# A planner that counts VectorE's pauses one behind the other, and inverse roots of eleven instructions

## The chip, the cores and the metric

The program runs on one core of one Trainium2 chip. The metric is the time of one execution on the device in microseconds (us). Five engines work side by side, each through its own list of instructions in the order in which the program emitted them: TensorE (PE, with PEld for the loading of weights), VectorE (DVE), ScalarE (ACT), GpSimd (POOL) and SyncE (SP), which starts most transfers.

## The reference

Two transformer blocks run one after the other over x, which is 2 x 1024 rows of 256, with 16 heads of 16.

- Block 1: norm, self-attention, residual; norm, cross-attention to 64 rows of context, residual; then a mixture of 8 experts. A router takes the two best experts of each row, each expert is a layer of 1024 with gelu, and the two answers are added with their gates.
- Block 2: norm, self-attention, residual; norm, cross-attention with a mask, residual; norm, a dense layer of 1024 with gelu, residual.

A norm in both blocks is (x - mean) / sqrt(var + 1e-5), then scale and shift:

```python
def _ln(x, g, b):
    m = x.mean(-1, keepdims=True)
    v = ((x - m) ** 2).mean(-1, keepdims=True)
    return (x - m) / jnp.sqrt(v + EPS) * g + b
```

## The kernel before

**Tiles and stages.** x lies in on-chip memory as 16 tiles of 128 rows. Four tiles are a unit, numbered 0 to 3, so that units 2 and 3 are the second batch. Self-attention runs in 128 cells a block (head by head, 128 keys to a cell), in which TensorE, VectorE (maxima of the scores) and ScalarE (exp) work in step. Everything else of the block is cut into steps which are put between the cells, and the steps that are left after the last cell run in a drain.

**What sets the order.** Four of the engines run in the order of emission, and the emission is planned in Python by `Stream`. A job is a generator (`Task`) which emits a few instructions and yields. A positive number is TensorE time that these take, a negative number a pause in which the job is not to be asked for its next step. `step` chooses between the cells, where a pause is rounded up to whole cells of 3.3 us. `rest` chooses in the drain: it keeps a clock `now` that only the positive numbers move, and takes of the jobs whose pause is over the one with the highest rank. A pause there begins at `now`, whatever else VectorE was given. None of these numbers reaches the chip. They set the order, and the chip's semaphores then hold each instruction until its data are there.

`rest` serves three stretches: the drain behind block 1's cells, the stretch in which block 2 begins while the last expert jobs run, and the drain behind block 2's cells.

**The jobs of block 1's drain**, with the lines by which the profile knows them:

- *Cross norm of unit 3* (`norm_task`, rank 67): `statistics` of four tiles on VectorE (L402, L403, tiles `st_c`, `mv_c`), `inverse_roots` (L385 to L393, `root_c`, `rs_c`), `center`, which makes the normed rows (L416, `xn_c`), and their turning on TensorE (L428) and ScalarE (L435). A pause of 3.4 stands behind the roots and one of 1.8 behind the first two tiles of `center`. At the end POOL adds a bias to x (L488).
- *Ask, weigh and share of unit 3* (ranks 30, 30, 50): queries (L1303), four groups of scores with their maxima (L1345 on TensorE, L1353, L1366 and L1367 on VectorE), `largest` (L1372), `weights` (L1382 and L1388, exp on ScalarE at L1393), `undivided` (L1442, L1452), `division` (L1467), and the output (L496, added to x at L504).
- *Dispatch of units 2 and 3* (`dispatch_task`, rank 70, tiles named `_m`): the same statistics and roots, the rows `xd_m` (L1576), their turning (L428), the router (L1589, L1599), the best two experts (L1602 to L1621, in two steps), the counts (L1629 to L1650), the gates (from L1655, with an exp at L1656), the places (L1675, L1676, two steps), and eight scattering transfers by POOL (L1684).
- *Find* (`find` with `Places.make`, rank 65): six small VectorE steps (L1697 to L1812) that say which expert each slot of 256 rows serves. SP then reads the numbers and fetches weights (L1872) and rows (L1864).
- *Slots 0 to 4* (ranks 10 to 6): turning of the fetched rows (L1934) with seven small VectorE instructions (L1940 to L1957), `first0` to `first3` (L1969, gelu on ScalarE at L1975), and four halves of `second` (L2000). Slot 0 may begin when units 0 and 1 are counted, the others when unit 2 is.
- *Context of block 2* (rank -20), which fills gaps (L1223, L1245).
- The last heads of self-attention (L888 to L914) and their projection (L496), on which the cross norm of unit 3 waits.

Fourteen instructions make the roots: two for a first guess, then three rounds of four. `helper()` gives POOL while `maxima[0]` is true, which is as long as VectorE has maxima to take, and VectorE after that.

Of the kernel before, what the change touches and what calls it, by code (L numbers as in the profile page):

```python
# [43 lines left out]
I32 = mybir.dt.int32  # L44
U32 = mybir.dt.uint32
AF = mybir.ActivationFunctionType
ALU = mybir.AluOpType
# [5 lines left out]
B, S, D, H, DH = 2, 1024, 256, 16, 16  # L53
# [5 lines left out]
EPS = 1e-5  # L59

GUESS = 0x5F3759DF
# [3 lines left out]
CELL = 3.3  # L65
# [66 lines left out]
W_B1, W_1, W_2, W_B2 = 0, 8, 2056, 4104  # L132
NFF = 4360

class Task:


# [7 lines left out]
class Stream:  # L145
# [63 lines left out]
                self.advance(t)  # L209
        assert mark in self.made, mark  # L210

    def rest(self, later, cell, mark=None):

        now, ready = 0.0, {t: (t.first - cell) * CELL for t in self.tasks}
        while (self.tasks or later) and (mark is None or mark not in self.made):
            for c in sorted(later):
                if (c - cell) * CELL <= now:
                    for go in later.pop(c):  # L220
                        go()
            tasks = [t for t in self.tasks if self.made.issuperset(t.after)]
            able = [t for t in tasks if ready.get(t, 0.0) <= now]
            if able:
                t = max(able, key=lambda t: (t.rank, -ready.get(t, 0.0)))
                cost = self.advance(t)
                if cost is not None:
                    now += max(0.0, cost)
                    ready[t] = now - min(0.0, cost) + (t.pause or 0.0)
            else:  # L230
                now = min([ready[t] for t in tasks] + [(c - cell) * CELL for c in later])
        return now
# [3 lines left out]
def two_blocks(  # L236
# [16 lines left out]
    nc = tc.nc  # L253
    const = ctx.enter_context(tc.tile_pool(name="const", bufs=1))
# [87 lines left out]
    def choice(layer, pool):  # L342
        for b in range(1 + layer):
            chosen[layer].append(pool.tile([P, 2, P], F32R, name=f"chosen{layer}{b}"))
# [26 lines left out]
    maxima = [True]  # L371
# [6 lines left out]
    def inverse_roots(rs, var, tag, pool, engine):  # L378


        n = rs.shape[1]
        v, r = [
            pool.tile([P, 8], F32, tag="root", name=f"root{i}_{tag}", bufs=4)[:, :n] for i in range(2)
        ]
        engine.tensor_scalar(v, var, EPS, None, ALU.add)  # L385
        engine.tensor_scalar(
            rs.bitcast(I32), v.bitcast(I32), -0.5, float(GUESS), ALU.mult, ALU.add
        )
        for _ in range(3):
            engine.tensor_tensor(r, rs, rs, ALU.mult)  # L390
            engine.tensor_tensor(r, r, v, ALU.mult)
            engine.tensor_scalar(r, r, -0.5, 1.5, ALU.mult, ALU.add)
            engine.tensor_tensor(rs, rs, r, ALU.mult)  # L393

    def statistics(src, nt, tag, pool=small, each=False, engine=None):


        st = pool.tile([P, 8, 6], F32, tag="st", name=f"st_{tag}", bufs=4)
        mv = pool.tile([P, 8, 2], F32, tag="mv", name=f"mv_{tag}", bufs=6)
        rs = pool.tile([P, 8], F32, tag="rs", name=f"rs_{tag}", bufs=6)  # L400
        for t in range(nt):
            nc.vector.bn_stats(st[:, t, :], src(t))  # L402
            nc.vector.bn_aggr(mv[:, t, :], st[:, t, :])  # L403
            if each or t % 2 == 1:
                yield -1.2
        inverse_roots(rs[:, :nt], mv[:, :nt, 1], tag, pool, engine or helper())
        yield -3.4 if engine is None else -4.4
        return mv, rs

    def center(src, pair, held, tag, pool=small):  # L410
# [30 lines left out]
    def norm_task(first, nt, ln, dst, tag, pool=small, held=None, engine=None):  # L441


        def src(t):
            return x_sb[:, first + t, :]

        if held is None:
            held = yield from statistics(src, nt, tag, pool, engine=engine)
        nxt = center(src, (0, 1), held, tag, pool)
        yield -1.8  # L450
        for t0 in range(0, nt, 2):
            xns, nxt = nxt, None
            if t0 + 2 < nt:
                nxt = center(src, (t0 + 2, t0 + 3), held, tag, pool)
            i, tp = turned(xns)
            affine(dst[:, :, t0 * P : (t0 + 2) * P], i, tp, ln)
            yield 1.0, 1.8
# [1105 lines left out]
    def dispatch_task(unit, pool, counted):  # L1563
# [7 lines left out]
        mv, rs = yield from statistics(src, 4, name)  # L1571
# [5 lines left out]
                xd[:, t, :D], src(t), mv[:, t, 0:1], rs[:, t : t + 1], ALU.subtract, ALU.mult  # L1577
            )
        lg = small.tile([P, 4, E], F32, tag="lg", name=f"lg_{name}")
        yield -5.0 if maxima[0] else -1.8  # L1580
        hT = pool.tile([P, 2, 512], F32, tag="dh", name=f"hT_{name}")
        for t0 in range(0, 4, 2):
            i, tp = turned([xd[:, t0 + n, :D] for n in range(2)])
# [26 lines left out]
        for k in range(2):  # L1610
            hot = hots[k]
            nc.vector.tensor_reduce(mx[:, k, :], lg, AX.X, ALU.max)
            nc.vector.tensor_tensor(hot, lg, mx[:, k, :].unsqueeze(2).to_broadcast(shape), ALU.is_equal)
            nc.vector.tensor_tensor(hot, hot, desc_b, ALU.mult)
            first = small.tile([P, 4], F32, tag="first", name=f"first_{name}{k}")
            nc.vector.tensor_reduce(first, hot, AX.X, ALU.max)
            nc.vector.tensor_tensor(hot, desc_b, first.unsqueeze(2).to_broadcast(shape), ALU.is_equal)
            yield -1.0
            if k == 0:
                nc.vector.scalar_tensor_tensor(lg, hot, -3.0e38, lg, ALU.mult, ALU.add)  # L1620
                nc.vector.tensor_scalar(  # L1621
                    xd[:, :, D + M_E0], first, -1.0, float(E), ALU.mult, ALU.add
                )
# [17 lines left out]
        else:  # L1641
# [1 line left out]
                before, before, inside.unsqueeze(2).to_broadcast([P, E, 4]), ALU.add  # L1643
            )
            nc.vector.tensor_tensor(inside, inside, upto[:, :, 3], ALU.add)
        yield -1.2
        i, pk = bank()
        pk = pk[:, : E * 4]
        nc.tensor.matmul(pk, lhsT=tri, rhs=chosen.rearrange("p e t -> p (e t)"), start=True, stop=False)
# [23 lines left out]
        for k in range(2):  # L1673
            mine = small.tile([P, 4, E], F32, tag="mine", name=f"mine_{name}{k}")
            nc.vector.tensor_tensor(mine, hots[k], place.rearrange("p e t -> p t e"), ALU.mult)  # L1675
            nc.vector.tensor_reduce(at[:, k, :], mine, AX.X, ALU.max)  # L1676
            yield -0.5
        counted()

        for t in range(4):  # L1680
# [36 lines left out]
    class Places:  # L1717
# [3 lines left out]
        def make(self, pool, name, n, had, caps, last):  # L1721
# [18 lines left out]
            nc.vector.memset(begin[:, m:], 0.0)  # L1740
            nc.vector.tensor_copy(end[:, : m - E], begin[:, E:m])
            nc.vector.tensor_copy(end[:, m - E :], caps[-1])
            yield -0.9
            upto = pool.tile([P, m], F32, tag="ntu", name=f"ntu_{name}", bufs=1)
            nc.vector.tensor_tensor(upto, end, begin[:, :m], ALU.subtract)
            nc.vector.tensor_tensor_scan(upto, ones[:, :m], upto, 0.0, ALU.mult, ALU.add)
# [17 lines left out]
                ALU.is_ge,  # L1764
            )
            self.who = const.tile([P, n], F32, name=f"who_{name}")
            yield -0.9
            row = pool.tile([P, n], F32, tag="row", name=f"row_{name}", bufs=1)
            past = pool.tile([P, n], F32, tag="past", name=f"past_{name}", bufs=1)
            nc.vector.tensor_reduce(self.who, over, AX.X, ALU.add)  # L1770
# [4 lines left out]
            self.at = const.tile([P, 2, n], I32, name=f"at_{name}")  # L1775
            nc.vector.tensor_scalar(row, self.who, float(E - 1), None, ALU.min)
            nc.vector.tensor_copy(self.at[:, 0, :], row)
            yield -0.9

            nc.vector.tensor_tensor(over, over, end.unsqueeze(1).to_broadcast(shape), ALU.mult)  # L1780
            nc.vector.tensor_reduce(row, over, AX.X, ALU.add)
            nc.vector.tensor_tensor(row, number, row, ALU.subtract)
            yield -0.9
            nc.vector.tensor_scalar(row, row, begin[:, 0:1], 256.0, ALU.add, ALU.mult)
            nc.vector.scalar_tensor_tensor(
                row, self.who, float(PART), row, ALU.mult, ALU.add
            )
            nc.vector.tensor_scalar(row, row, float(NROWS - 256), None, ALU.min)
            nc.vector.tensor_copy(self.at[:, 1, :], row)
            yield -0.9  # L1790
            if last:
                rest = more[:, 1:2]
                nc.vector.scalar_tensor_tensor(
# [20 lines left out]
    class Mixture:  # L1814
# [211 lines left out]
        def find(self, units):  # L2026

            last = units == len(NFULL)
            had = self.places[-1].tiles if self.places else None
            end = NSLOT if last else NFULL[units]  # L2030
            n = end - (self.ends[-1] if self.ends else 0)
            if units == 2:
                self.caps = expert_tiles("2", (FULL, ANY))
                caps = 2 * self.caps[:1]
            else:

                caps = [self.caps[last], *expert_tiles(f"{units}", (OVER, ANY) if last else (FULL,))]
            yield -0.9
            pool = self.epool[1] if self.epool else const
            places = Places()  # L2040
            yield from places.make(pool, f"{units}", n, had, caps, last)
            self.places.append(places)
            self.ends.append(end)
            yield 0.3
            yield -3.0

            self.load(1)
# [141 lines left out]
    def block(layer, tail, heads=None, beside=None):  # L2189

        pools = {}
# [6 lines left out]
        if layer == 0:  # L2198
            open_pools()
            context_places(0, pools["cpool"])  # L2200
            choice(0, pools["cpool"])
            bias_out.extend(pools["dpool"].tile([P, D], F32, name=f"bias_out{i}") for i in range(2))
        made, ys, ready = [], [], {}

# [69 lines left out]
        stream, later = self_attention(layer, tail, heads, arrive, extra, when_ready, around)  # L2274
# [13 lines left out]
    mixture = Mixture(slotw, epool)  # L2288
    stream, later, _, _ = block(0, tail)
# [26 lines left out]
    with ExitStack() as passing:  # L2316

        xpool = passing.enter_context(tc.tile_pool(name="xpool", bufs=1))
        stream.add(
            context_task(1, *context_load(1, xpool), xpool), 6.0, mark="context1", rank=-20  # L2320
        )
        stream.rest(later, 64 * B + 2)
    tail.close()
    hpool = ctx.enter_context(tc.tile_pool(name="hpool", bufs=1))
    load_attention(2)
# [189 lines left out]
```

## Time and profile before

| | us |
|---|---|
| time before, median of 3 runs | 1524.51 (1523.71 to 1528.62) |
| the profiled execution's own time | 1523.15 |
| its span, first to last instruction | 1521.2 |
| TensorE busy | 1433.5 (94%) |
| VectorE busy | 980.6 (64%) |
| ScalarE busy | 920.1 (60%) |
| block 1's drain, about | 542 to 686 |
| block 2's beginning beside the last expert jobs, about | 786 to 894 |
| block 2's drain, from about | 1378 |

All times in the text are us from the start of the span. The page and the views name an instruction by engine and line, and by the names of what it writes and reads. The number in square brackets is the engine's idle time ahead of it, followed by what ended that. The granted TensorE clock is given in tenths on the page and as a share in the table of windows. The order is fixed when the program is built, so an engine that waits for one instruction also holds back all that was emitted behind it on that engine, ready or not.

### The profile page before, as it was taken

Reading aid. Unit: us, or ns where it says so; the run is one execution under the profiler, and the core shown is the slowest. Engines: PE = TensorE matmul, PEld = TensorE weight load, DVE = VectorE, ACT = ScalarE, POOL = GpSimd, SP = SyncE. Lnnn points to the kernel's source line nnn. Section 1 sums busy time; section 2 is a strip of 40 time slices with the busy share of each in tenths; the row PEclk is TensorE's granted clock in tenths of the full one; section 3 lists DMA queues with packets and bytes.
Section 4 is the critical chain, followed back from the end, with each engine's and each line's share of the span. In section 5 each row is a group of like instructions: output and inputs, shape, how many; then the busy total and the mean of one; then the engine's idle time right before and its main releaser. Section 6 shows DMA issues by size and latency. Waiting matters only on the chain. (4 is left out here: it accounts for less than half of the span.)

```text
span 1521.2 us, 29858 instructions
## 1 busy us (share of the span) xinstructions
PE 1433.5 (94%) x11172; PEld 833.4 (55%) x11172; DVE 980.6 (64%) x2221; ACT 920.1 (60%) x1797; POOL 356.3 (23%) x492
## 2 busy tenths in 40 slices
PE   6999999999899968999999998999999999999998
PEld 3444444444445445788888664444454454446676
DVE  7967788978878564531115768877886886944210
ACT  3477788777677825323323346877877777783411
POOL 2311234325143022031112023211322322411010
PEclk9999999999999988999999999999999999999999
DMA  9663112111011030566556541232211112000000
GB/s 335 234 246 107 64 58 78 36 45 44 29 58 34 5 115 29 213 242 229 191 198 237 166 149 65 63 106 71 64 50 52 44 36 97 30 9 29 8 14 28
DMA packets 69157, 148.71 MB, mean 98 GB/s; under 512 B 12842, under 2 KB 26668, under 8 KB 68620
## 3 DMA queue, kind: packets, MB, share of 16 engines
q1 hardware_dynamic: 65788, 137.86, 26.3%
q0 software_dynamic: 3216, 8.85, 1.6%
q8 instruction: 91, 1.49, 0.4%
q14 instruction: 62, 0.51, 0.1%
HBM read 94.32 MB, written 51.99 MB: 96 GB/s over the span
## 5 line engine op out<-in xcount | busy, mean ns | idle before, releaser
L945 DVE TENSOR_REDUCE mx_s<-banks 128x1 f32<-128x512 f32 x1024 | 634.7, 681 | 125.8 <-PE banks L976 118.8
L954 ACT ACTIVATE pt_s<-banks 128x512 f32<-128x512 f32 x1024 | 535.1, 603 | 123.0 <-PE banks L976 118.9
L1032 PE MATMUL banks<-pt_s,v_s 128*32 128x512 f32 x2048 | 260.7, 603 | 10.2 <-ACT pt_s L954 4.5
L1045 POOL TENSOR_TENSOR acc_s<-acc_s,part_s 128x512 f32<-128x512 f32 x130 | 166.9, 1284 | 417.5 <-ACT part_s L1044 416.9
L976 PE MATMUL banks<-qb_s,eps_both 32*128 32x512 f32 x1024 | 198.1, 390 | 0.0
L2000 PE MATMUL banks<-w_slot,h_s 128*128 128x256 f32 x560 | 125.1, 380 | 0.4 <-DVE spread L1011 0.4
L1032 PEld LDWEIGHTS banks<-pt_s,v_s 128*32 128x32 f32 x2048 | 49.8, 109 | 124.6 <-ACT pt_s L954 65.1
L1044 ACT COPY part_s<-banks 128x512 f32<-128x512 f32 x145 | 87.0, 600 | 47.3 <-PE banks L1032 44.7
L2000 PEld LDWEIGHTS banks<-w_slot,h_s 128*128 128x128 f32 x560 | 105.4, 190 | 15.6 <-DVE spread L1011 0.8
L2009 DVE SCALAR_TENSOR_TENSOR ys<-banks,gate,b 128x256 f32<-128x256 f32 x35 | 16.9, 482 | 132.2 <-PE banks L2000 132.2
L976 PEld LDWEIGHTS banks<-qb_s,eps_both 32*128 32x128 f32 x1024 | 95.5, 184 | 8.7
L1975 ACT ACTIVATE h_s<-banks,w_slot 128x256 f32<-128x256 f32 (+1 forms) x104 | 41.1, 446 | 86.1 <-issue 50.3
L2015 POOL DMA_INDIRECT results<-ys,to x35 | 34.1, 973 | 226.2 <-DVE ys L2009 177.4
L1969 PE MATMUL banks<-xsT,w_slot 128*128 128x256 f32 (+1 forms) x416 | 84.9, 357 | 0.9 <-ACT xsT L435 0.9
L1969 PEld LDWEIGHTS banks<-xsT,w_slot 128*128 128x128 f32 x416 | 70.9, 190 | 12.0 <-issue 2.8
L2153 PE MATMUL banks<-hT_f,w_ff 128*128 128x512 f32 x128 | 57.0, 596 | 0.0
L2165 PE MATMUL banks<-w_ff,h_f 128*128 128x256 f32 x256 | 56.6, 379 | 0.0
L1353 DVE TENSOR_REDUCE mx_c<-banks 128x4 f32<-128x256 f32 (+1 forms) x96 | 44.1, 504 | 18.4 <-PE banks L1345 18.3
L706 PE MATMUL banks<-xT_s,w_att 128*128 128x512 f32 x104 | 50.9, 613 | 3.2 <-ACT pt_s L954 2.3
L1975 ACT ACTIVATE h_s<-banks,spare 128x256 f32<-128x256 f32 (+1 forms) x56 | 21.7, 444 | 52.5 <-PE banks L1969 35.0
L2165 PEld LDWEIGHTS banks<-w_ff,h_f 128*128 128x128 f32 x256 | 48.2, 190 | 7.2 <-issue 1.0
L2156 ACT ACTIVATE h_f<-banks,w_ff 128x512 f32<-128x512 f32 x32 | 21.9, 687 | 48.6 <-PE banks L2153 48.6
(379 smaller groups left out, 2913.8 us busy)
## 6 DMA issues: line engine op xcount, KB each, us to landing
w_slot<-in_ff_w_dram SPq DMA_DIRECT2D x40, 576.0 KB
sorted_rows<-fill SPq DMA_DIRECT2D x36, 520.0 KB
w_slot<-in_ff_w_dram SPq DMA_DIRECT2D x26, 514.0 KB
whole<-acc_s SPq DMA_DIRECT2D x30, 256.0 KB
spare<-in_ff_w_dram SPq DMA_DIRECT2D x14, 514.0 KB
q_parts<-spare SPq DMA_DIRECT2D x13, 512.0 KB
KS<-k_parts SPq DMA_DIRECT2D x12, 512.0 KB
k_parts<-spare SPq DMA_DIRECT2D x10, 512.0 KB
```

Source lines behind the costliest of these rows:

```text
L706: nc.tensor.matmul(p, lhsT=w[:, at + k * D + pair * P : at + k * D + (pair + 1) * P], rhs=xT[b][:, k, blk * 512 : (blk + 1) * 512], start= ...
L945: nc.vector.tensor_reduce(to, sc, AX.X, ALU.max)
L954: nc.scalar.activation(pt, sc, AF.Exp, scale=SCALE)
L976: nc.tensor.matmul(sc, lhsT=lhsT, rhs=rhs, start=now[0] == 1, stop=last)
L1032: nc.tensor.matmul(o[32 * j : 32 * (j + 1), :], lhsT=V_flat[b][:, at : at + 32], rhs=exps.pop((cell, j)), start=(cell == cells[0]), stop=( ...
L1044: nc.scalar.copy(part, o)
L1045: helper().tensor_tensor(acc[h], acc[h], part, ALU.add)
L1969: nc.tensor.matmul(ph[:, n, :], lhsT=w[:, at : at + P], rhs=xT[:, k, :], start=(k == 0), stop=(k == 1),)
L1975: nc.scalar.activation(h1[:, f, :rows], ph[:, n, :], AF.Gelu, bias=w[:, W_B1 + f : W_B1 + f + 1])
L2000: nc.tensor.matmul(py, lhsT=h1[:, f, h * P : (h + 1) * P], rhs=w[:, f * D : (f + 1) * D], start=(f == 0), stop=(f == 7),)
L2153: nc.tensor.matmul(ph, lhsT=w1[:, at : at + P], rhs=hT[:, k, :], start=(k == 0), stop=(k == 1))
L2165: nc.tensor.matmul(py[:, n, :], lhsT=h1[:, f, t * P : (t + 1) * P], rhs=w2[:, f * D : (f + 1) * D], start=(f == 0), stop=(f == 7),)
```

## The change

It has five parts.

1. `Late` is a kind of number. Steps that end in VectorE work yield `Late(-c)` in place of `-c`.
2. `rest` can be called with `queued=True`, as it now is for block 1's drain alone. It then keeps a second clock, `vector`: a `Late` pause begins at the end of the last one, if that is after `now`.
3. Pauses become shorter where the roots are on VectorE: 2.3 for 3.4 behind the roots, 0.8 for 1.8 behind the first rows of a norm, 1.6 for 1.8 behind the dispatch's rows. This holds for all three stretches, and between the cells too.
4. The dispatch's two steps for the best two experts become one, and so do its two steps for the places, where there are no maxima to take.
5. On VectorE the roots take eleven instructions: two, then three rounds of three. `find` may also use another pool for its small tiles if it starts ahead of the expert jobs' pools.

```diff
+class Late(float):
+    pass
...
-        now, ready = 0.0, {t: (t.first - cell) * CELL for t in self.tasks}
+        now, vector, ready = 0.0, 0.0, {t: (t.first - cell) * CELL for t in self.tasks}
...
                     ready[t] = now - min(0.0, cost) + (t.pause or 0.0)
+                    if queued and isinstance(cost, Late):
+                        ready[t] = vector = max(now, vector) - cost
...
+        if engine is nc.vector:
+            engine.tensor_scalar(v, var, EPS, None, ALU.add)
+            engine.tensor_scalar(
+                rs.bitcast(I32), v.bitcast(I32), -0.5, float(GUESS), ALU.mult, ALU.add
+            )
+            for _ in range(3):
+                engine.tensor_tensor(r, rs, rs, ALU.mult)
+                engine.scalar_tensor_tensor(r, r, -0.5, v, ALU.mult, ALU.mult)
+                engine.scalar_tensor_tensor(rs, r, 1.5, rs, ALU.add, ALU.mult)
+            return
...
             if each or t % 2 == 1:
-                yield -1.2
+                yield Late(-1.2)
         inverse_roots(rs[:, :nt], mv[:, :nt, 1], tag, pool, engine or helper())
-        yield -3.4 if engine is None else -4.4
+        yield -4.4 if engine else -3.4 if maxima[0] else Late(-2.3)
...
         nxt = center(src, (0, 1), held, tag, pool)
-        yield -1.8
+        yield -1.8 if maxima[0] else Late(-0.8)
...
-        yield -5.0 if maxima[0] else -1.8
+        yield -5.0 if maxima[0] else Late(-1.6)
...
-            yield -1.0
+            if k == 1 or maxima[0]:
+                yield Late(-1.0 if maxima[0] else -2.0)
...
-        yield -1.2
+        yield Late(-1.2)
         i, pk = bank()
...
-            yield -0.5
+            if k == 1 or maxima[0]:
+                yield Late(-0.5 if maxima[0] else -0.7)
...
-            yield -0.9
+            yield Late(-0.9)
...
-            pool = self.epool[1] if self.epool else const
+            pool = self.epool[1] if self.epool else self.scratch
...
+            mixture.scratch = pools["dpool"]
...
-        stream.rest(later, 64 * B + 2)
+        stream.rest(later, 64 * B + 2, queued=True)
```

The line with `-0.9` stands for all six such lines of `find` and `Places.make`. The last hunk is the call of `rest` behind block 1's cells.

More of the change, by code (lines that the diff above doesn't have):

```diff
@@ L210, in until, with rest @@
         assert mark in self.made, mark
-    def rest(self, later, cell, mark=None):
-        now, ready = 0.0, {t: (t.first - cell) * CELL for t in self.tasks}
+    def rest(self, later, cell, mark=None, queued=False):
+        now, vector, ready = 0.0, 0.0, {t: (t.first - cell) * CELL for t in self.tasks}
         while (self.tasks or later) and (mark is None or mark not in self.made):
@@ L1766, in make @@
             self.who = const.tile([P, n], F32, name=f"who_{name}")
-            yield -0.9
+            yield Late(-0.9)
             row = pool.tile([P, n], F32, tag="row", name=f"row_{name}", bufs=1)
@@ L1777, in make @@
             nc.vector.tensor_copy(self.at[:, 0, :], row)
-            yield -0.9
+            yield Late(-0.9)
             nc.vector.tensor_tensor(over, over, end.unsqueeze(1).to_broadcast(shape), ALU.mult)
@@ L1782, in make @@
             nc.vector.tensor_tensor(row, number, row, ALU.subtract)
-            yield -0.9
+            yield Late(-0.9)
             nc.vector.tensor_scalar(row, row, begin[:, 0:1], 256.0, ALU.add, ALU.mult)
@@ L1789, in make @@
             nc.vector.tensor_copy(self.at[:, 1, :], row)
-            yield -0.9
+            yield Late(-0.9)
             if last:
@@ L2037, in find @@
                 caps = [self.caps[last], *expert_tiles(f"{units}", (OVER, ANY) if last else (FULL,))]
-            yield -0.9
-            pool = self.epool[1] if self.epool else const
+            yield Late(-0.9)
+            pool = self.epool[1] if self.epool else self.scratch
             places = Places()
```

## The prediction, made before the changed kernel was run

> **What bounds the kernel now.** Read first: the engines' busy times and the granted clock on the page.
>
> ```profile
> PE 1433.5 (94%) x11172; PEld 833.4 (55%) x11172; DVE 980.6 (64%) x2221; ACT 920.1 (60%) x1797; POOL 356.3 (23%) x492
> ...
> PEclk9999999999999988999999999999999999999999
> ```
>
> TensorE is busy for all but 88 us of 1521.2, and its clock drops in slices 15 and 16 (570 to 646 us) alone. Second, the table of windows there (columns: length, busy time and instructions of PE, PEld, DVE, ACT, POOL, then granted clock, DMA).
>
> ```profile
> 557.00:569.00 12.00, 0.09 (x1) 0.00 (x0) 10.59 (x55) 0.85 (x4) 0.00 (x0) 0.63 0.50 188
> 569.00:594.00 25.00, 20.10 (x126) 13.84 (x127) 15.48 (x55) 12.64 (x22) 2.83 (x3) 0.84 0.00 1
> 594.00:624.00 30.00, 27.17 (x191) 20.42 (x190) 11.43 (x44) 11.34 (x18) 8.47 (x9) 0.94 0.57 211
> 645.00:720.00 75.00, 74.34 (x357) 65.21 (x356) 21.51 (x102) 24.90 (x58) 18.60 (x25) 1.00 0.67 230
> ```
>
> For 12 us VectorE alone works; from 645 us TensorE is full. Nothing later gives the loss back, and no transfer holds TensorE there, so a microsecond won ahead of 645 is won at the end. Third, TensorE's waits between 540 and 660 us:
>
> ```profile
> PE banks L428 <- DVE xn_c L416: 11.9, 1, 11.9
> PE banks L428 <- DVE xd_m L1576: 2.4, 2, 1.8
> PE banks L1372 <- DVE spread L1367: 2.3, 1, 2.3
> PE banks L1452 <- issue: 1.9, 2, 1.0
> ```
>
> The long one is for the normed rows of unit 3. Fourth, VectorE's timeline ahead of them:
>
> ```profile
> 555.78 0.17 DVE L1780 TENSOR_TENSOR over<-over,end 128x16 f32<-128x16 f32 x1
> ...
> 560.96 0.16 DVE L385 TENSOR_SCALAR root_c<-mv_c 128x4 f32<-128x4 f32 x1
> ...
> 564.70 0.40 DVE L402 BATCH_NORM_STATS2 st_m<-x_sb 128x6 f32<-128x256 f32 x1
> ...
> 565.88 0.17 DVE L385 TENSOR_SCALAR root_m<-mv_m 128x4 f32<-128x4 f32 x1
> ...
> 568.54 2.33 DVE L416 TENSOR_SCALAR xn_c<-x_sb,mv_c,rs_c 128x256 f32<-128x256 f32 x4
> ```
>
> VectorE never pauses from 555.8 to 573. The roots that TensorE waits for are done at 563.6, but the dispatch of unit 2 (`_m`) stands before the rows: the planner let both pauses run at once. Last, ScalarE around 600 us, where exp and gelu alternate, each switch a table load:
>
> ```profile
> 597.82 1.28 ACT L1393 ACT_TABLE_LOAD   x1
> ...
> 601.20 1.28 ACT L1975 ACT_TABLE_LOAD   x1
> ...
> 606.94 1.28 ACT L1393 ACT_TABLE_LOAD   x1 [1.15 <-PE banks L1388]
> ```
>
> **The new order.** Yields fix it, so it can be worked out. Taking the drain's jobs through the old rule gives the old trace's sequence. Through the new one, from the norm's roots on:
>
> ```
> VectorE old: roots c | stats m 0-3 | roots m | rows c 0-3 | slot 0 | xd
> VectorE new: roots c | stats m 0-1 | rows c 0-1 | stats m 2-3 | rows c 2-3 | slot 0 | roots m | xd
> TensorE old: turn c, slot 0, turn c, turn xd, first0, L1589, L1303, L1599, L1303, 3 scores, counts,
>   score, first1, largest, first2, weights, first3, undivided, weights, division, undivided
> TensorE new: turn c, slot 0, turn c, first0, first1, turn xd, L1303 x2, L1589, score, L1599, 3 scores,
>   first2, counts, largest, first3, weights, undivided, weights, second0, division, undivided
> ```
>
> In the last cells, the dispatch of unit 1 comes a cell earlier at its rows (2.3 rounds up to one cell, 3.4 to two) and gains more where steps join: its first scattering and `find`'s first step move from the drain to the last cell. Block 2's two stretches keep their order, but for one turning of a norm that moves ahead of one block of the dense layer; its rows (1386.5) are done 4 us before. There only roots shorten, beside a full TensorE: nothing.
>
> **Part by part.**
>
> *A, the long wait.* Gone from the chain ahead of the rows: one `find` step (L1780 to L1782, 555.78 to 556.26, 0.48), three of fourteen instructions at 0.2 (0.6), half the dispatch's statistics (564.70 to 565.88, 1.18), its roots (565.88 to 568.54, 2.66). Together 4.9: TensorE goes on at 564.1, not 569.0. L1785, of the new instructions' kind, takes 0.16 like the old ones. The dispatch's remaining statistics (1.06) still stand ahead of the rows. Slot 0's fetched rows are in at 564.1 by the DMA packets, and their numbers come earlier now; a wait there is priced below.
>
> *B, the dispatch's rows.* The 1.8 ahead of turning them is covered by first0 and first1 (3.5). Against that the second pair of rows now stands behind statistics: 0.8 to 1. Slot 0's L1945 took 1.19 where 0.16 is usual, beside POOL's L488, which will run among these too. Sum -0.8; ends -1.8 and +0.4.
>
> *C, the scores.* L1303 now goes ahead of the router, so the best two experts fall among the maxima. From the first score to `largest` VectorE has four pairs of maxima at 1.28, two copies at 0.42, the best two (582.31 to 585.0, 2.7), the counts (1.1), and 0.8 before it can begin: 10.5. TensorE has 6.0 to do: it waits 4.5 where it waited 0.44, 0.30 and 2.33. +1.4; ends 0 and +2.8. No queue takes new waits; behind these wait first3 and the weights.
>
> *D, exp and gelu.* Before, both `undivided` sat behind a gelu-to-exp switch: the first took 5.0 for 1.9 of work (1.93 of that gaps without a cause shown), the second 0.9 of idling and 3.3. Now first3 comes ahead of the first weights, and nothing with gelu between the two. The first loses 2.5 (1.28, four exp in 2.06, less L1697) and keeps its gaps; the second, behind second0, nothing: 4.4 for 5.4. -1.0; ends -2.9, if the gaps go, and +2.5, if the second still waits.
>
> *E, the last cells.* The dispatch's rows (L1576, 1.37) now come ahead of a cell's maxima, so the next scores wait up to 1.4; a wait of 0.68 for `hT_m` (519.26) goes. +0.7; ends -0.7 and +1.4.
>
> *F, the clock.* Granted clock in a stretch and the one behind it (PE alone):
>
> ```profile
> 590.74:594.15 3.41, 1.08 (x7) 1.00 0.00 0
> 594.15:597.56 3.41, 3.41 (x13) 0.50 0.24 83
> ```
>
> Half speed follows a stretch that was a third busy, though its longest gap was 2.33. Behind the long wait it lasted from 560.0 to 577.1. The excess then: twenty turning matmuls took 5.2 (8 took 1.09 at 516.1, so 2.7), first0 2.72 for 1.99: 3.2; behind the short one 1.2 (L1969 at 593.7, 3.20 for 1.99). A wait of 7 us still halves it, but first0 and first1 make the next stretches full: 2.1, and 1.5 behind C's waits, 3.6 for 4.4. -0.8; ends -4.4 (all gone) and +3.
>
> [...]
>
> *Moved past other queues.* SP's list is empty between its last head transfer (492) and slot 0's (554), so earlier fetches pass nothing. POOL's eight scatterings, 10 us, start sooner and end before its bias sums. `find`'s other pool does not come into use: its first step alone falls into the cells.
>
> Sum: -4.9 - 0.8 + 1.4 - 1.0 + 0.7 - 0.8 = -5.4. The profiled execution's 1523.15 (span 1521.2 and 1.95 around it) would be 1517.8, its span 1515.8. The median lies 1.4 above that execution: 1524.5 - 5.4 = 1519.1.
>
> **The rivals.**
>
> *Rows of slot 1 come late (same).* Slots 1 and 2 now stand right behind unit 3's output, as second3 has moved ahead of it. Before, the packets of the three fetches ended 11.2 after the numbers (609.2 to 620.4). With the forecast's lead slot 1 could begin at 618.1; the second `undivided` ends 10.4 of work before that, and VectorE needs 1.8 to the numbers: 609.5. With the same lag the rows are there at 620.7: 2.6 back, 1521.7. For it: fetches queue in turn. Against it: the lag contains 2.2 MB of weights, which are now asked for some 5 us earlier.
>
> *The rows are not ahead after all (same).* Had the dispatch's roots still come first, only six root instructions and a `find` step would go (1.7), with C against it: 1524.2. Against it: in the table its second statistics must wait for the first's pause.
>
> *Half clock through the drain (slower).* The stretch from 570.3 to 573.7 was 46% busy and the clock stayed down. If the waits of B, C and D leave stretch after stretch from 564 to 600 under half, each of some ten costs up to 1.7. Eight cost 13.7 in place of the forecast's 3.6: -5.4 + 10.1 = +4.7, 1529.2. It decides from six on, where the gain is used up. Against it: slowed matmuls fill a stretch better, and first0 with first1 are 3.5 without a wait.
>
> **How the numbers follow.** 0.3% is 4.6 us, about what a measurement of this kernel tells from no change. Forecast (A to F as they stand) 0.70, of which a tenth stays within 4.6; late rows 0.10; rows not ahead 0.08; half clock 0.12. Faster by over 0.3%: 0.60; within: 0.28 (0.10 + 0.10 + 0.08); slower: 0.12. The forecast's own range is 1514.8 (D's and F's lower ends half met) to 1522. Leaving out the slower case's 0.12 and some 0.06 below, the range is 1514.8 to 1526.0.
>
> **What would show it.** A: the first L428 on `xn_c` near 564, its wait near 7; `xn_c` rows in VectorE's list between `st_m` pairs. B: no wait on `xd_m` above 0.5 there. C: waits on `chosen_m` near 2.6 and on `spread` near 1.5. D: one table load fewer before slot 1, no wait ahead of the second `undivided`. F: half clock back to full by 571. Slot 1's turning 6 to 8 us ahead of 623.6, and that lead kept to block 2. Wrong if the long wait keeps over 10 us, or if the lead at slot 1 is lost behind it.

## The result, and the profile after

The changed kernel took 1535.79 us (median of 7 runs, 1533.79 to 1540.81) against 1524.63 for the kernel before beside it (7 runs): a ratio of 1.0071, with a 95% interval of 1.0055 to 1.0087. It is slower by 11.2 us, where 5.4 less were forecast. The profiled execution took 1535.3 with a span of 1533.3, 12.1 longer than before. The lines named below stand 16 to 18 further down the file than before: L444 is the old L428, L1952 the old L1934, L1483 the old L1467.

The page of the kernel after, engines and granted clock:

```profile
PE 1443.7 (94%) x11172; PEld 841.1 (55%) x11172; DVE 975.7 (64%) x2202; ACT 916.8 (60%) x1794; POOL 355.8 (23%) x492
...
PEclk9999999999999988899999999999999999999999
```

At this scale one sees only a TensorE that needed 10 us more for the same instructions, and a third slice with a lower clock. The waits of TensorE between 540 and 660 us (in total, times, longest) say where:

```profile
PE banks L1952 <- DMA xs<-sorted_rows: 6.6, 1, 6.6
PE banks L444 <- DVE xn_c L432: 4.3, 1, 4.3
PE banks L1483 <- DVE count L1719: 3.7, 1, 3.7
PE banks L1666 <- DVE chosen_m L1646: 2.9, 1, 2.9
PE banks L1239 <- ACT kvT L1231: 2.6, 1, 2.6
```

The long wait did fall, from 11.9 to 4.3, and the wait ahead of the dispatch's rows is gone. Three waits are new: 3.7 and 2.6 at the drain's very beginning, and 6.6 for the rows of slot 1. Laying the same instruction of both traces side by side gives the account (before, after, difference): first sum of the last self-attention share 542.07, 546.02, +3.95; end of the context's keys and values (L1245, now L1261) 557.09, 569.71, +12.6; first `xn_c` turned 569.01, 574.03, +5.0; slot 1 turned 623.55, 635.35, +11.8. The difference then stays to the end. Of the first +3.95, 1.74 was there at cell 114 (484 to 487 us), before anything had changed place. So two things went wrong, one at 547 to 560, worth 8.7, and one at 629 to 635, worth 6.6.

**The first loss, read closely.** TensorE's timeline after:

```profile
544.71 1.06 PE L1468 MATMUL banks<-pt_c,picks 128*32 128x128 f32 x32
...
546.02 1.08 PE L904 MATMUL banks<-acc_s,picks 128*64 128x512 f32 x4
547.03 1.15 PE L910 MATMUL banks<-acc_s,picks 128*32 128x128 f32 x16
551.84 2.05 PE L1483 MATMUL banks<-inv_c,picks 128*128 128x128 f32 x8 [3.66 <-DVE count L1719]
```

and VectorE's:

```profile
550.73 0.96 DVE L1477 RECIPROCAL inv_c<-banks 128x128 f32<-128x128 f32 x1 [5.28 <-remote]
551.61 0.10 DVE L1719 TENSOR_SCALAR count<-banks 128x8 f32<-128x8 f32 x1
...
556.58 0.96 DVE L918 RECIPROCAL inv_s<-banks 128x128 f32<-128x128 f32 x1 [3.76 <-remote]
```

The wait is put down to `count`, but TensorE needed `inv_c`, which VectorE made just ahead of it. VectorE had been idle for 5.28 and began at 550.73, though its input, L1468's last matmul, had ended at 545.77. `remote` says that the signal came without a sender that the trace could match. The reader of L910 (ended 548.18) began at 556.58, 8.4 late. The matmuls were done; the news of it was late. Beside it GpSimd wrote the second dispatch's rows, eight indirect DMAs (GpSimd's timeline):

```profile
544.79 1.08 POOL L1702 DMA_INDIRECT sorted_rows<-xd_m,at_m  x1 [1.39 <-DVE mine_m L1692]
...
553.77 0.96 POOL L1702 DMA_INDIRECT sorted_rows<-xd_m,at_m  x1 [0.30 <-issue]
```

The kernel before shows the same, in another place. Its writes began at 543.7, when the share's sums were done, and fell beside the projection, from VectorE's timeline before:

```profile
552.28 0.69 DVE L504 TENSOR_TENSOR x_sb<-x_sb,banks 128x512 f32<-128x512 f32 x1 [1.58 <-PE banks L496]
555.17 0.69 DVE L504 TENSOR_TENSOR x_sb<-x_sb,banks 128x512 f32<-128x512 f32 x1 [1.18 <-remote]
```

These add banks whose matmuls ended at 550.18 and 551.90: 2.1 and 3.3 late. TensorE had more of the projection to do and lost nothing there.

**The second loss.** SP's issues after (SPq, a group's first issue and how long the group took):

```profile
614.83 11.36 SPq L1890 DMA_DIRECT2D w_slot<-in_ff_w_dram  x8
626.76 0.87 SPq L1890 DMA_DIRECT2D spare<-in_ff_w_dram  x2
628.62 2.14 SPq L1882 DMA_DIRECT2D xs<-sorted_rows  x3
```

VectorE's last step for the numbers of these rows:

```profile
620.52 0.17 DVE L1807 CAST at<-row 128x4 int32<-128x4 f32 x1
```

and SP's issues before:

```profile
608.24 2.25 SPq L1872 DMA_DIRECT2D w_slot<-in_ff_w_dram  x4
611.07 2.46 SPq L1864 DMA_DIRECT2D xs<-sorted_rows  x3
614.03 1.10 SPq L1872 DMA_DIRECT2D w_slot<-in_ff_w_dram  x2
```

The numbers of the rows were ready at 620.7. The fetches now stand behind ten weight loads instead of four, and from 618.6 to 625.3 the seventh load waits for slot 0 to give its buffer back. In `find` the slots become known ahead of its last pause; in that pause a half of an expert ends and calls `load`, which asks for every weight that has a place, and `rows` comes only then.

### The profile page after: what moved, and what is told of

It is laid out like the page before. It is cut to its first block, busy times and chain, and to the rows that moved or that the text cites. A ratio compares the mean times of both kernels' runs of the same rounds, so it can differ in the third digit from the quotient of the medians.

```text
span 1533.3 us, 29848 instructions
## 1 busy us (share of the span) xinstructions
PE 1443.7 (94%) x11172; PEld 841.1 (55%) x11172; DVE 975.7 (64%) x2202; ACT 916.8 (60%) x1794; POOL 355.8 (23%) x492
## 5 line engine op out<-in xcount | busy, mean ns | idle before, releaser
L1987 PEld LDWEIGHTS banks<-xsT,w_slot 128*128 128x128 f32 x416 | 72.1, 193 | 12.1 <-issue 2.8
```

The source lines that it names most:

```text
L1987: nc.tensor.matmul(ph[:, n, :], lhsT=w[:, at : at + P], rhs=xT[:, k, :], start=(k == 0), stop=(k == 1),)
```

## The experiments

Theory S: the row writes hold up TensorE's signals (the news that a matmul is done), and the new order puts the share's sums, a chain of handovers, into their 10 us. Theory for the second loss: SP's order alone. Rival Q: the waits come from VectorE's queue, as the profile names them, or from the order clock. A run is compared with the kernel before on the same chip. There were four such comparisons, each on another chip (10, 9, 8 and 7): e1 to e4, e5 to e8, e9 to e12 and e13 to e16. The kernel before took 1519.3, 1520.1, 1526.9 and 1526.7 us in them.

**e1, row writes held.** The rows' last column is copied later, so the writes, which read it, start later.

```diff
-        nc.vector.tensor_copy(xd[:, :, D + M_TOK], ...)
+        if unit != 1:
+            nc.vector.tensor_copy(xd[:, :, D + M_TOK], ...)
...
         counted()
+        if unit == 1:
+            yield -2.0
+            nc.vector.tensor_copy(xd[:, :, D + M_TOK], ...)
```

> The kernel after, with one copy of VectorE (the token numbers of the second dispatch, 0.16 us) moved behind the reciprocal of the self-attention share (inv_s), so that the eight row writes of that dispatch, which read it, start about 4 to 6 us later; TensorE's order and everything else stay. Theory S (TensorE's signals are held up while a dispatch's row writes run): the sums for the two shares (L1468, L904, L910) are told to VectorE and ScalarE within 0.1 us of their last matmul, where the kernel after had them 4.9 to 8.4 us late; the waits of 3.66 us ahead of L1483 and 2.63 us ahead of L1239 fall below 1 us each; the projection ends 7 to 9 us sooner, some 2 to 4 us of it given back where the writes now lie beside the projection; slot 1's rows stay late by 5 to 7 us. Time 1528 to 1532 us, ratio to before 1.002 to 1.005. Rival Q (the wait is the one the profile names, VectorE's queue with count and its new order, or the code block that TensorE fetched at 545.9): the order on VectorE and the code are the same, so both waits stay above 2 us and the time stays within 1.5 us of 1535.8.

Ratio 1.0037 (1.0023 to 1.0051). Both early waits were gone, but e2 and e4, which do not hold the writes, had none either: no reader of TensorE started over 0.9 us late in any trace of e1 to e8. This run tells nothing of S; e13 does.

**e2, rows ahead of weights on SP.**

```diff
             self.ends.append(end)
+            if units == 3:
+                self.load(1)
+                self.nrows = NFULL[units]
+                self.load(0)
             yield 0.3
```

> The kernel after, with the loads of the rows of slots 1 to 3 issued on SP right behind the weights of slot 1 rather than behind those of slots 2 and 3; the order on TensorE, VectorE, ScalarE and GpSimd stays. Theory: slot 1's rows are late because SP issued them at 628.6, behind a weight load that waited until 625.3 for slot 0 to free its buffer, and not because their numbers (VectorE, 620.7) were late; they would be issued at about 621, land by 628, and the wait of 6.61 us ahead of L1952 falls below 1.5 us, with no wait for slot 2's weights later: 5 to 7.5 us saved, 1528 to 1531 us. Rival: the weights that are now later are waited for in slot 2 (above 2 us), or the rows wait for their packets behind the weights' as before, and less than 2 us is saved. The early waits of 3.66 and 2.63 us stay.

Ratio 0.9969 (0.9955 to 0.9983): faster than before. SP's issues in e2:

```profile
602.95 2.25 SPq L1892 DMA_DIRECT2D w_slot<-in_ff_w_dram  x4
607.83 2.16 SPq L1884 DMA_DIRECT2D xs<-sorted_rows  x3
610.52 2.34 SPq L1892 DMA_DIRECT2D w_slot<-in_ff_w_dram  x4
```

The rows are asked for 0.6 after their numbers (607.2), TensorE does not wait for them, and the weights that are later now are waited for nowhere. The early waits, which the expectation kept, were absent.

**e3, the two places in two steps again** (undoes one value of the change).

```diff
-            if k == 1 or maxima[0]:
-                yield Late(-0.5 if maxima[0] else -0.7)
+            yield Late(-0.5)
```

> The kernel after with one value of the change undone: the two searches for a row's place in a dispatch are again two steps with a pause between them, so that seven of the second dispatch's eight row writes wait until VectorE has taken the sums of the context share; SP's order is that of the kernel before, so slot 1's rows are again issued ahead of slot 2's weights. Theory S: the waits ahead of L1483 and L1239 fall below 1.5 us each (one row write alone runs beside the share's sums), slot 1's rows are waited for by less than 1 us, and the rest of the change is worth what was forecast: 1518 to 1524 us, ratio 0.996 to 1.000. Rival Q (the order clock itself, or the shorter pauses, set the first share behind other work on VectorE): waits above 2 us at the same two places, 1527 us or more.

Ratio 0.994 (0.9917 to 0.9964), the lowest of all here, though its interval overlaps that of e2. SP's order is the old one again, and the rows are in time. The early waits are absent as in e2, so this run did not test S either.

**e4, the order clock off** (`queued=False`).

> The kernel after with the order clock of VectorE's pauses off and all new values, merged steps and roots kept. VectorE's order up to the projection is the one of the kernel after, SP's that of the kernel before. Theory S: the early waits stay (2.5 to 4 us ahead of L1483 and 1.5 to 3 us ahead of L1239, signals of L1468 over 3 us late), the rows of slot 1 are in time, 1526 to 1531 us. Rival Q (the order clock makes the early waits): they are gone, 1518 to 1524 us.

Ratio 1.0016 (1.0001 to 1.0031), without the early waits. Taken alone that would speak for Q; e5, which has the clock on and no early waits, takes it back. So does e2, beside e4 on the same chip: it has the order clock on and no early waits, and with the rows in time in both its ratio is 0.9969 against 1.0016, with intervals that do not meet.

**e5 and e6, both kernels again.**

> The kernel after itself, beside the kernel before on one chip, for its trace. In the first comparison TensorE's signals came 0.9 to 8.4 us late in both kernels while a dispatch's row writes ran; in the four runs since, none came later than 0.7 us there. Theory S2 (late signals belong to the chip or the moment, late rows to the order): with signals in time there is no wait above 1 us ahead of L1483 and L1239, slot 1's rows are still waited for by 5 to 7.5 us, and the ratio to before lies between 1.000 and 1.004 rather than at 1.0071. Rival (the new order itself brings the signals late, and the edits of the other runs had removed that): both early waits are back, 2 us or more each, ratio 1.005 to 1.009.

> The kernel before itself, for its trace on the chip of e5. Theory S2: no signal of TensorE over 0.7 us late in the row writes of the second and third dispatch (0.9 to 3.5 us in the first comparison); VectorE adds the projection's banks as they come, so the first xn_c is turned 2 to 4 us sooner after the projection, the long wait is 8 to 10 us rather than 11.9, and the drain up to slot 1 is 3 to 6 us shorter. Rival: signals late as in the first comparison, long wait 11 to 12.5 us.

The ratio of e5 is 1.0019 (1.0008 to 1.0031). TensorE's waits, e6 first:

```profile
PE banks L428 <- DVE xn_c L416: 9.3, 1, 9.3
PE banks L428 <- DVE xd_m L1576: 2.4, 2, 1.8
PE banks L1372 <- DVE spread L1367: 2.3, 1, 2.3
```

and e5:

```profile
PE banks L1952 <- DMA xs<-sorted_rows: 7.4, 1, 7.4
PE banks L444 <- DVE xn_c L432: 4.3, 1, 4.3
PE banks L1666 <- DVE chosen_m L1646: 2.9, 1, 2.9
PE banks L1388 <- DVE spread L1383: 1.2, 1, 1.2
```

With signals in time the same kernel has no early waits, and the kernel before has a long wait of 9.35 instead of 11.92. At slot 1 the kernel after is 2.70 behind (621.44 against 618.74), which is 7.41 of waiting for rows and a lead of 4.71. Both expectations of S2 held.

**e7, the roots alone** (the kernel before with part 5).

> The kernel before with only the roots of VectorE in eleven instructions instead of fourteen; TensorE's order is unchanged. Theory: each root chain on VectorE is 0.6 us shorter, and only the one behind the projection lies on the path: the long wait is 0.5 to 0.7 us shorter than that of e6, the time is 0 to 1 us less, ratio 0.999 to 1.0005. Rival (three table-free instructions less also let the drain's later roots count): 1.5 to 3 us, ratio 0.998 to 0.999.

Ratio 0.999 (0.9977 to 1.0003). The long wait was 8.12 against e6's 9.35: 1.23 less, twice what was expected, because the dispatch's roots stood ahead of the norm's rows too, so two chains became shorter.

**e8, the old pauses of the norm** (3.4 and 1.8 for 2.3 and 0.8).

> The kernel after with the old pauses behind norm's roots and rows (3.4 and 1.8 instead of 2.3 and 0.8); order clock, merged steps and short roots stay, SP's order is that of the kernel before. Theory (the rows of slot 1 are the loss, the order of norm's rows a gain of some us): slot 1's rows in time, no wait above 1.5 us ahead of its turning; the long wait some 1 to 3 us longer than with the new pauses, because a find step or dispatch statistics stand ahead of norm's rows on VectorE again; ratio 0.995 to 1.000. Rival (the new norm pauses are worth nothing): as e3 within 1 us, 0.993 to 0.995.

Ratio 0.9974 (0.9963 to 0.9986). Slot 1's rows were in time. TensorE waited 3.8 for slot 0's rows and then 2.7 for `xn_c`, 6.5 where e5 waits 4.3; but from cell 114 to the drain it took 2.0 less than e5. So in these two traces the new pauses win 2.1 in the waits and lose 2.0 in the cells.

**e9 and e10, more steps parted again.** e9 has the dispatch's old pauses throughout (1.8, 1.0 twice, 0.5 twice), e10 the old steps for the two experts alone.

> The kernel after with all of the dispatch's joined steps parted again at their old pauses (1.8, 1.0 twice, 0.5 twice); order clock, norm's new pauses and short roots stay; SP's order is that of the kernel before. Theory (the gain is norm's rows right behind their roots, the loss is SP's order): slot 1's rows in time, the long wait 4 to 5.5 us, the cells' second half without the 1.5 us that the earlier rows of the second dispatch cost there; ratio 0.991 to 0.996. Rival (the joined steps carry a part of the gain): the waits for the dispatch's best two experts and its spread come to 6 us or more between the projection and slot 1, ratio 0.996 to 0.999.

> The kernel after with only the choice of the two experts parted into two steps again (1.0 twice); the rest of the change stays, SP's order is that of the kernel before. Theory: slot 1's rows in time, long wait 4 to 5.5 us, ratio 0.992 to 0.997, within 3 us of e3. Rival: as the kernel after plus the rows' gain only, 0.9965 to 0.998.

0.9976 (0.9957 to 0.9996) and 0.9992 (0.9982 to 1.0001). Signals were late again in these comparisons, and the long wait was 7.0 in both: banks of the projection were told up to 1.2 late.

**e11, e3 again, and e12, the kernel after once more.**

> The kernel of e3 again, for a narrower interval: 0.992 to 0.996 where TensorE's signals are in time. On a chip with signals late as in the first comparison, theory S2 gives 0.992 to 0.999, since seven of the eight row writes start behind the share's sums, as in the kernel before.

> The kernel after once more, a look for TensorE's signals in the row writes: either none over 0.7 us late and a wait of 6 to 8 us for slot 1's rows alone (as in e5), or the two early waits of the first comparison as well.

e11 came to 0.9989 (0.9973 to 1.0005), and TensorE still waited 3.3 ahead of L1483. What was expected of e3 and e11, that seven of the eight row writes come behind the share's sums, did not hold: four were issued (551.48 to 555.40) before the signal for L1468, whose matmuls ended at 552.45, came at 556.66. e12 took 1538.57, 1.0077 of the kernel before beside it, (one run) and showed all three waits again: 3.6, 3.2 and 6.1.

**e13 to e16.**

> The kernel of e1 again (the second dispatch's row writes held until VectorE has the sums of the self-attention share). If TensorE's signals are late on this chip (the kernel before then shows 1523 us or more), theory S gives the sums of the two shares on time (under 0.3 us late), the waits of 3.6 and 2.6 to 3.2 us ahead of L1483 and L1239 below 1 us each, and a ratio of 1.001 to 1.005 where the kernel after had 1.0071 and 1.0077; signals late instead in the projection, by 1 to 3 us. Rival (the lateness follows the code or the sums themselves, not the row writes): both waits stay, ratio 1.006 to 1.009. If signals are prompt: 1.002 to 1.005 as in e1.

> The kernel of e2 again (rows of slots 1 to 3 fetched ahead of the weights of slots 2 and 3). With late signals: the early waits stay and the rows' wait goes, ratio 1.001 to 1.004, some 5 to 8 us under the kernel after. With prompt signals: 0.995 to 0.998 as in e2.

> Both edits at once, e1's and e2's. Theory (two losses, each with its own cause): the gains add; with late signals 0.994 to 0.999, with prompt ones 0.995 to 0.999 (the holding then costs up to 1 us because slot 0's rows are written later). Rival (one loss hides the other): no better than the better of e13 and e14.

> The kernel of e9 again (all joined steps of the dispatch parted). With prompt signals 0.992 to 0.996, like e3; with late ones 0.996 to 0.9995 as in e9.

e13 speaks for S. In it VectorE's order is that of the kernel after but for the one copy, and the writes begin later. GpSimd's timeline:

```profile
549.04 1.08 POOL L1706 DMA_INDIRECT sorted_rows<-xd_m,at_m  x1 [5.69 <-DVE begin L1759]
```

VectorE, where the lateness is now on L520:

```profile
545.79 0.96 DVE L1477 RECIPROCAL inv_c<-banks 128x128 f32<-128x128 f32 x1 [0.40 <-PE banks L1468]
...
560.42 0.69 DVE L520 TENSOR_TENSOR x_sb<-x_sb,banks 128x512 f32<-128x512 f32 x1 [3.67 <-remote]
```

TensorE, without idle time:

```profile
547.55 1.16 PE L1483 MATMUL banks<-inv_c,picks 128*128 128x128 f32 x8
...
553.44 3.62 PE L512 MATMUL banks<-w_att,ot_s 128*128 128x256 f32 x16
```

The writes start 4.25 later than in the kernel after. The share's sums are told within 0.1, L1483 waits for nothing, and instead the third bank of the projection, done at 557.05, is told at 560.4. The lateness stays in the time of the writes, though not in all of it: five signals between 549.1 and 555.4 were prompt. The early stretch is back to 14.5 (23.7 in the kernel after), and 3.3 of that is given back at the long wait (7.6). Ratio 1.0022 (1.0001 to 1.0044). e14, on the same chip without the holding, keeps the early waits (3.7 and 3.2) and loses the rows', with a ratio of 1.0016 (0.9996 to 1.0036). TensorE's timeline in e14:

```profile
553.34 1.39 PE L1483 MATMUL banks<-inv_c,picks 128*128 128x128 f32 x8 [3.70 <-DVE count L1721]
```

e15 has both edits: 0.9978 (0.9954 to 1.0001). From 1.0071 the holding takes 0.0049 and the rows 0.0055; together they take 0.0093. Within this one comparison, e15 against e14 gives 0.0038 for the holding and e15 against e13 gives 0.0044 for the rows. With intervals of about 0.002 to either side, that fits two separate losses that add. e16, e9 again, is at 0.9978 (0.9963 to 0.9993).

e9 and e16 are one kernel, and it is 0.2% faster than the kernel before in two comparisons with late signals; it was not run with signals in time. There the lowest ratio is that of e3, at 0.994, which with late signals (e11) cannot be told from the kernel before.

## Why the prediction was wrong

*The step that failed first* is "Moved past other queues", with the rival "Rows of slot 1 come late". The rival had the place right and the price wrong: 2.6 against 6.6 to 7.4. It let the fetches be issued as soon as their numbers are there, as before. But a job that is moved takes with it the DMAs that its end issues: `second` was moved ahead, its end calls `load`, and that put the weights of slots 2 and 3 ahead of the rows on SP. One of those waits for a buffer. No single part of the change does it: e3, e4, e8, e9 and e10 each take back one part, the order clock in e4, and in each the rows of slot 1 were in time. The prediction looked at SP's list for 492 to 554, and not for 608 to 629. e2 shows, as far as its interval tells, that this is all of it where signals are in time: with the rows ahead the ratio is 0.9969 (0.9955 to 0.9983), and the forecast of 1519.1 is 0.9965 of 1524.5.

*The step that was missing* is the handovers beside the row writes. The prediction said of the eight writes that they "start sooner and end before its bias sums", and priced GpSimd's time, not what the other engines do meanwhile. Before, they began when the share's sums were done; after, while these were being made, since the sums came 3.95 later than before and the writes 1.1. The trace of before had hints: VectorE idle for `remote` ahead of L504 at 555.17, and in D "1.93 gaps without a cause shown", which are absent in e6, where signals were in time.

*The terms*, by e5 against e6, where signals were in time:

| term | forecast | measured | how |
|---|---|---|---|
| A, long wait | -4.9 | -5.0 | 9.35 to 4.33 |
| B, dispatch's rows | -0.8 | -1.8 | wait gone; the second pair of rows waited for nothing |
| C, scores | +1.4 | +1.2 | 3.07 to 4.27 |
| D, exp and gelu | -1.0 | -0.4 | both `undivided` with the waits ahead of them, 6.95 to 6.56 |
| E, last cells | +0.7 | +1.75 | 1.93 in the cells, 0.18 of it back in the drain |
| F, clock and the rest | -0.8 | -0.45 | what is left of -4.71 |
| rows of slot 1 | 0 | +7.41 | wait ahead of L1952 |

The sum without the last line is -4.7 for -5.4. That it came so near is in part luck: B is 1.0 better than forecast, D and E are 0.6 and 1.05 worse. A is right to 0.1 on these traces; in the first comparison it was -7.6, since late signals had lengthened the long wait before. C's wait on `chosen_m` was 2.92 for 2.6, that on `spread` 1.21 for 1.5. D: table loads fell from six to four between the long wait and slot 1, and the second `undivided` waits for nothing, but the first, which had no wait in e6, now has one of 1.22 and takes 3.39 for 2.65; the gaps around it in the trace of before are absent in e6. E was too small: the wait for VectorE's maxima at 512 is 0.94, within what was said, and a stretch at half clock follows it (513.4 to 516.9); that this cost the rest is argued, not shown. The slower rival, half clock through the drain, did not come. Two readings of the prediction were off, and the sum does not rest on them: slices 15 and 16 of the page are 532 to 608 us, not 570 to 646, and the wait for slot 0's rows that A says is priced below has no price there. No such wait came in the kernel after; e8 had one of 3.8.

The first comparison's +12.1 of span then is: +1.7 ahead of any moved step, +2.2 in the cells, +8.7 in the early drain, -7.6 in the long wait, +6.6 for the rows, +0.5 in the rest. The stretches at half clock that follow the early waits are part of the 8.7; the windows after (length, then busy time of PE, PEld, DVE, ACT and POOL, granted clock, DMA):

```profile
548.14:551.55 3.41, 0.04 (x1) 0.00 (x0) 0.82 (x1) 0.00 (x0) 2.50 (x4) 1.00 0.24 88
551.55:554.97 3.42, 2.90 (x12) 2.53 (x12) 1.12 (x7) 0.59 (x1) 2.57 (x3) 0.50 0.30 108
554.97:558.38 3.41, 1.01 (x9) 1.01 (x10) 1.73 (x7) 0.58 (x1) 0.00 (x0) 1.00 0.11 39
558.38:561.79 3.41, 3.41 (x15) 3.05 (x14) 2.03 (x11) 1.50 (x4) 0.00 (x0) 0.50 0.00 0
```

Each stretch in which TensorE had little to do is followed by one at half speed, as the prediction read it. The Trainium skill (TensorE: Matmul & The Clock Gate, HAM oscillation) gives as a rule that TensorE should have no idle gaps above about 3.4 us. The first pair fits that, with a gap of 3.66 from 548.18 to 551.84; the second does not, as the longest gap in it is 2.63.

What stays open: why signals were in time in the comparisons of e1 to e8 and late in the first one and in e9 to e16, with the same kernels. Nothing in a kernel decides it, and as each of the four later comparisons ran on another chip, the chip and the moment cannot be told apart. How a row write holds a signal up was not found either. Whether fewer bytes a row would hold them up less was not tried.

## What to carry to other kernels

When a plan of order moves a job, follow what its end issues onto the DMA queue, and look for the one load there that waits for a buffer: all that stands behind it is late by that wait, however early its data are ready. Keep chains of handovers between engines out of the time in which indirect writes run, and put long work of one engine there (where signals came late, this was worth 0.0038 of the time, e15 against e14); a wait that the profile puts down to `remote`, or to an engine long done, is the sign to look for. Where a ratio moves by half a per cent from one comparison to another, compare traces of both kernels taken side by side before a cause is named.

## What the hardware showed

- While the eight indirect row writes of a dispatch ran, TensorE's results were told to VectorE and ScalarE up to 8.4 us after the last matmul, in three of five comparisons and in both kernels. The traces keep the time of each signal. In the ten traces of those three comparisons (before, after, e9 to e16), every signal that came more than 0.9 us late, ahead of the program's end, belongs to a matmul that ended between the first row write of a dispatch and about 2 us behind the record of its last. In the eight traces of e1 to e8 no signal was that late. Not every signal in the time of the writes is held: in e13 five were prompt in the first 6.3 us, and then three came together from 560.39 to 560.58. VectorE's own instructions were not slower (0.96 for the reciprocal with and without), and its result reached TensorE at once: `inv_c` was done at 551.69 and L1483 began at 551.84.
- GpSimd's record of such a write is not the move. The Trainium skill (Perfetto Trace Analysis, DMA Instruction — SWDGE (GPSIMD)) says that the profiler's end is that of the descriptors. The trace agrees: the last record of the kernel after ends at 554.73, the last packet at 555.82.
- Half clock also came behind a stretch that was busy for the most part: 510.0 to 513.4 in e5 has TensorE busy for 2.37 of 3.40, with a longest gap of 0.94, and 513.4 to 516.9 ran at 0.51. In e6 the same stretch has 3.18 busy and full speed behind it. The stretch in e5 held waits and matmuls of 32 rows; where the bound lies is not known.
- Ahead of every moved step, kernels differed by some us in one execution: cell 114 began at 484.4 in e5 and e6, at 487.1 in e4 and at 490.6 in e11, with 10.2, 6.8, 13.7 and 23.9 us at half clock before it. A difference between two single executions is therefore read here from one instruction to another, and not from the start of the span.
